# Pairing the products of a seven-product query projection in PSUM banks, and dealing its matmuls out among those of P.V

## The chip, the core and the metric

The kernel runs on one core of a Trainium2 chip. The metric is the device time of one execution in microseconds (us). Before the change it is 1138.15 us, the median of five runs (1136.66 to 1140.64).

## The reference

The input x is 1024 rows of 512 features, all in float32. First comes causal attention with 32 query heads that share 8 key/value heads (groups) of width 128, then a small feed-forward part with routed low-rank experts, each behind a layer norm and added to its input:

```python
q = (hidden_states @ w_q).reshape(B, S, Hkv, g, D)      # 1024 x 512 by 512 x 4096
k = (hidden_states @ w_k).reshape(B, S, Hkv, D)
v = (hidden_states @ w_v).reshape(B, S, Hkv, D)
scores = jnp.einsum('bqhgd,bkhd->bhgqk', q, k) * scale
...
probs = jax.nn.softmax(scores.astype(jnp.float32), axis=-1).astype(q.dtype)
attn = jnp.einsum('bhgqk,bkhd->bqhgd', probs, v)
return attn.reshape(B, S, Hq * D) @ w_o
```

The change concerns the first line, and the order in which its matmuls stand beside those of the last einsum, "P.V".

## The kernel before

**Blocks.** The work is cut into 64 blocks (g, t): group g of 8, and t of 8 tiles of 128 query rows. Groups 0 to 5 run through t = 0 to 7 one after the other (blocks 0 to 47); groups 6 and 7 follow in another order. Block i makes four quarters of scores, j = 0 to 3 (`scores`, L452): a quarter is 32 query rows for each of the group's four heads, 128 rows in all, against the 128t + 32(j+1) keys that the causal mask leaves. TensorE writes a quarter to a tile `s` of two PSUM banks (two such tiles). VectorE adds the mask to the last 32 columns (L472) and takes the negated maximum (L474), ScalarE takes the exponential and its sum (L479), GpSimd the reciprocal (L481). The quarter before is then finished (`finish_scores`): ScalarE multiplies by the reciprocal (L487) and VectorE transposes in 32 x 32 squares into a tile T (L490). After the fourth quarter 16 transfers on SP's queue bring T into a tile K, keys on the partitions (`to_keys`, L500). T and K have one buffer each for even and for odd t.

**P.V** of block i-2 runs in block i (`weighted_values`, L510): t+1 matmuls of 512 columns into one bank `po`, of which there is one. All of them read all parts of K. ScalarE copies the result to attnT (L516).

**The query projection.** A pair is two neighbouring blocks (t even, t odd) of a group, 256 query rows. The odd block i projects the queries of the next pair, m = i // 2 + 1. For m = 2 to 24 (23 pairs, `QW`; blocks 3, 5, ... 47) this is `project_q_halves`, L379: the product of a 2 x 2 block matrix of weights with a 2 x 2 block matrix of x in seven products in place of eight. Product number i multiplies a weight combination `weights["sq", 0][i]` (a11, a12, s4, a22, s1, s2, a21) with a combination of x `weights["tx"][i]` (b11, b21, b22, t4, t1, t2, t3). The sums s1, s2, s4 are made by GpSimd once a group (`combine_q`), t1 to t4 once a pair (`combine_x`, the tile `tx`). A product is four pieces: two halves c of 128 output rows by two steps k of 128 features, each a matmul of 128 columns. It fills half a PSUM bank. Banks come from a pool `pm` of three, which all projections share.

The order is written out by hand: `order` gives for each step n the product, the bank b = 0 to 3 and the half x of it. `merge(n)` is called when step n is complete: at n = 0 ScalarE copies product 0 to both halves of the first half tile of qT (L398); at n = 2 VectorE adds bank 1 (two products, L400); at n = 3 to 6 it adds products by halves (L402, L404, L405, L407, L409). Bank 0 is thus read at n = 0 with one product in it and gets its second at n = 3; bank 2 is read at n = 4 and gets its second product at n = 5.

**Order on TensorE.** For each block the main loop (L810) collects lists of pieces, each with its columns: `q` (the query projection), `other` (key and value projections), `pv`, and in even blocks `o_pair` (the output projection). `weave` deals two lists out by columns. `then` is q in front and the rest behind, and it is run in four shares by columns, one after each quarter of scores. In an odd block of groups 0 to 5, `o`, `o_pair`, `begins` and `ends` are empty, so `rest` is `other` (four value pieces of 256 columns in groups 2 and 4 and in t = 5 and 7 of group 0, nothing in the odd groups) and then `pv` (8, 2, 4 or 6 pieces for t = 1, 3, 5, 7). `combine_o` prepares weights on GpSimd (four subtractions) at the end of block t = 2 of each group from group 1 on; the weights of the next group's queries are loaded at t = 6, those of its output projection at t = 5, on ScalarE's queue. The framework adds the waits; TensorE's order is kept as written (`keep`), that of the other engines is set when the kernel is built.

Of the kernel before, what the change touches and what calls it, by code (L numbers as in the profile page):

```python
# [9 lines left out]
F32 = mybir.dt.float32  # L10
I32 = mybir.dt.int32
AF = mybir.ActivationFunctionType
ALU = mybir.AluOpType
AX = mybir.AxisListType

P = 128
# [6 lines left out]
def kernel(  # L23
# [32 lines left out]
    nc = tc.nc  # L56
# [3 lines left out]
    R = w_q.shape[1] // D // G  # L60
# [5 lines left out]
    PQ = 2 * P  # L66
    SQ = P // R
    NSUB = P // SQ
# [10 lines left out]
    act = ctx.enter_context(tc.tile_pool(name="act", bufs=2))  # L79
# [12 lines left out]
    QW = range(2, N2 // 2 + 1)  # L92
# [4 lines left out]
    def matmul(*args, **kw):  # L97
        keep(nc.tensor.matmul(*args, **kw))  # L98
# [84 lines left out]
    two = (nc.sync, nc.scalar)  # L183
# [77 lines left out]
    def bank(name):  # L261
        return ps_m.tile([P, 512], F32, tag="pm", name=name)
# [38 lines left out]
    vs, kTs, qTs = {}, {}, {}  # L301
# [77 lines left out]
    def project_q_halves(m):  # L379


        g, u = pairs[m]
        hk = KC // 2
        pm = {}

        def half(e, h):

            return both(e)[:, h]

        def both(e):  # L390
            q = qTs[g, u][:, ts(e, NSUB), :, :]
            return q.rearrange("p s (x h) q -> p x s (h q)", x=2)

        def merge(n):
            if n == 0:
                qTs[g, u] = act.tile([P, PQ // SQ, R, SQ], F32, tag="qT", name=f"qT_{g}_{u}")
                one = pm[0][:, 0].unsqueeze(1)
                nc.scalar.copy(both(0), one.to_broadcast([P, 2, NSUB, 2 * SQ]))  # L398
            elif n == 2:
                nc.vector.tensor_tensor(both(0), pm[1], both(0), ALU.add)  # L400
            elif n == 3:
                nc.vector.tensor_tensor(half(1, 0), pm[0][:, 1], half(0, 1), ALU.add)  # L402
            elif n == 4:
                nc.vector.tensor_tensor(half(0, 1), pm[2][:, 0], half(0, 1), ALU.add)  # L404
                nc.vector.tensor_tensor(half(1, 1), pm[0][:, 1], half(0, 1), ALU.add)  # L405
            elif n == 5:
                nc.vector.tensor_tensor(half(1, 0), pm[2][:, 1], half(1, 0), ALU.add)  # L407
            elif n == 6:
                nc.vector.tensor_tensor(half(0, 1), pm[3][:, 0], half(0, 1), ALU.add)  # L409


        order = ((0, 0, 0), (1, 1, 0), (5, 1, 1), (4, 0, 1), (6, 2, 0), (2, 2, 1), (3, 3, 0))

        def piece(n, c, k):
            i, b, x = order[n]
            if c == k == 0:
                if x == 0:
                    whole = bank(f"pq_{g}_{u}_{b}")
                    pm[b] = whole.rearrange("p (x s n) -> p x s n", x=2, s=NSUB)
            assert weights["sq"] == (g,)  # L420
            matmul(
                pm[b][:, x, :, ts(c, SQ)],
                weights["sq", 0][i][:, k, ts(c, D)],
                weights["tx"][i][:, k, :].rearrange("p (s q) -> p s q", q=SQ),
                start=(k == 0),
                stop=(k == hk - 1),
            )
            if c == 1 and k == hk - 1:
                merge(n)

        return [
            (P, lambda n=n, c=c, k=k: piece(n, c, k))
            for n in range(7)
            for c in range(2)
            for k in range(hk)
        ]
# [90 lines left out]
    def project_o(g, t):  # L527


        def finish(pm):  # L530
            nc.vector.tensor_tensor(acc[t], pm, acc[t], ALU.add)
            attnT.pop((g, t))
            ffn_norms(t)

        def term(j):
            return attnT[g, t][:, ts(j, P)], weights["o", g][:, j, :]

        return chained(
            lambda: bank(f"pO_{g}_{t}"), [lambda j=j: term(j) for j in range(R)], finish
        )  # L540
# [68 lines left out]
    def reload_x(t):  # L609
        xt = state["x", t] = ffn.tile([P, H], F32, tag="x", name=f"xr_{t}")  # L610
        load(xt, x[ts(t, P), :])
# [78 lines left out]
    def ffn_store(t):  # L690
        load(out[ts(t, P), :], acc[t])
# [4 lines left out]
    def projections(i):  # L696


        g, t = blocks[i]
        q, other = [], []  # L700
        m = i // 2 + 1
        if i == 0:
            later["q"] = project_q(*pairs[m])
            q = later["q"][: 2 * KC]
        elif i == 1:
            q = later["q"][2 * KC :]
        elif i % 2 and m < len(pairs):
            q = project_q_halves(m) if m in QW else project_q(*pairs[m])
        if i < N2:
            if t == 2:  # L710
                other += project_k(g, 1)
            if t == 6:
                other += project_k(g + 1, 0)
            if g == 0 and t < 2:
                other += [(P * KC, lambda n=TPB + 2 + t: input_turn(n))]
                other += project_v(0, 2 + t)
            elif g % GV == 0 and (g or t >= TPB):
                other += project_v(g // GV, t)
        else:
            n = i - N2  # L720
            for k, what in ((0, (G - 1, 0)), (2, (G - 2, 1)), (3, (G - 1, 1))):
                if n == k:
                    other += project_k(*what)
            for t in {0: (0,), 1: (1,), 2: (2, 3), 3: (4, 5), 4: (6, 7)}.get(n, ()):
                other += project_v(g // GV, t)
        return q, other

    def loads(i):

        g, t = blocks[i]  # L730
        m = (i + 1) // 2 + 1
        if i % 2 == 0 and m < len(pairs):
            for j in range(2):
                load_q(pairs[m][0], j)
        if i < N2:
            if t == 3:
                load_k(g + 1)
            if t == 5 and g + 1 == G - 2:
                load_k(G - 1)
            if t == 6 and (g + 1) % GV == 0:  # L740
                for j in range(2):
                    load_v((g + 1) // GV, j)
            if t == 5:
                load_o(g + 1)
        elif i == N2 + 3:
            load_o(G - 1)
        elif i == N2 + 4:
            load_base("wk", (0, 1))
        elif i == N2 + 5:
            load_base("wv", (2, 3))  # L750
# [15 lines left out]
    def weave(a, b):  # L766

        na, nb = sum(c for c, _ in a), sum(c for c, _ in b)
        merged, at, bt, b = [], 0, 0, list(b)
        for c, f in a:  # L770
            merged.append((c, f))
            at += c
            while b and (bt + b[0][0] / 2) * na <= at * nb:
                bt += b[0][0]
                merged.append(b.pop(0))
        return merged + b
# [21 lines left out]
    def complete(i, *behind):  # L798


        for e in range(2):
            k = i - behind[e % len(behind)]
            if 0 <= k < N and k % 2 == e and blocks[k][0] == G - 1:
                return [blocks[k][1]]
        return []

    def attend(i):
        return weighted_values(*blocks[i])

    for i in range(N):  # L810
        loads(i)
        for t in complete(i, 2):
            reload_x(t)
        for t in complete(i, 7, 8):
            ffn_store(t)
        q, other = projections(i)
        pv = attend(i - 2) if i >= 2 else []
        o, o_pair, ends, begins = [], [], [], []
        for t in complete(i, 3):
            o = project_o(*blocks[i - 3])  # L820
        if i % 2 == 0 and i >= 4 and blocks[i - 4][0] < G - 1:
            o_pair = project_o_pair(*pairs[i // 2 - 2])
        for t in complete(i, 6, 7):
            ends = sum(ffn_out(t), [])
        for t in complete(i, 5):
            begins = ffn_router(t)

        rest = o + weave(o_pair, begins[1:] + other + pv)
        then = begins[:1] + q + ends[:-1] + rest[:4] + ends[-1:] + rest[4:]
        for n in range(NSUB):  # L830
            scores(*blocks[i], n)
            run_share(then, n, NSUB)
            if i % 2 == 0 and n < 2 and i // 2 + 1 in QW:
                (combine_x, combine_q)[n](i // 2 + 1)
        if i == NT:
            prepare_ffn()

        if i >= NT and blocks[i - 2][1] == 0 and blocks[i - 2][0] < G - 1:
            combine_o(blocks[i - 2][0])


    c, d, e, f = (blocks[k][1] for k in (N - 6, N - 5, N - 2, N - 1))
# [60 lines left out]
```

## Time and profile before

| | |
|---|---|
| runs, median (lowest to highest) | 1138.15 us (1136.66 to 1140.64) |
| profiled execution | 1136.66 us, span 1134.9 us |
| mean granted TensorE clock | 0.990 |
| score matmuls (768 records) | 276.3 us |
| P.V matmuls (576 records) | 277.9 us |
| query matmuls of 128 columns (1288 records) | 173.3 us |
| VectorE adds of the 23 projections, L400 to L409 | 15.6 us at 679 ns, the other five groups 9.5 to 9.8 us each at 415 to 424 ns |
| ScalarE copies, L398 | 13.3 us at 579 ns |
| transfers of K, 16 a block | 0.59 us apart on SP's queue, landing 1.7 to 2.5 us after their issue as a rule |

The times of one profiled execution are used for durations; its own time stands in the table beside its span, which runs from its first to its last instruction. A matmul in float32 shows as two records. The end of a matmul is modelled in the records, so their starts say more than their durations; times "at" some number are us from the start of the span.

### The profile page before, as it was taken

Reading aid. Unit: us, or ns where it says so; the run is one execution under the profiler, and the core shown is the slowest. Engines: PE = TensorE matmul, PEld = TensorE weight load, DVE = VectorE, ACT = ScalarE, POOL = GpSimd, SP = SyncE. Lnnn points to the kernel's source line nnn. Section 1 sums busy time; section 2 is a strip of 40 time slices with the busy share of each in tenths; the row PEclk is TensorE's granted clock in tenths of the full one; section 3 lists DMA queues with packets and bytes.
Section 4 is the critical chain, followed back from the end, with each engine's and each line's share of the span. In section 5 each row is a group of like instructions: output and inputs, shape, how many; then the busy total and the mean of one; then the engine's idle time right before and its main releaser. Section 6 shows DMA issues by size and latency. Waiting matters only on the chain.

```text
span 1134.9 us, 14168 instructions
## 1 busy us (share of the span) xinstructions
PE 1073.6 (95%) x4388; PEld 716.6 (63%) x4388; DVE 696.7 (61%) x1423; ACT 449.7 (40%) x962; POOL 331.3 (29%) x649
## 2 busy tenths in 40 slices
PE   8899999999999999999999999899999899999896
PEld 7666666666676666666776666656677456466453
DVE  4476656766566566666566655766336756666755
ACT  2544434444344433444344433444234353343400
POOL 5523334232242424232242424331131111112210
PEclk9999999999999999999999999999999999999998
DMA  6035432446125431455225351464334644453220
GB/s 206 22 93 134 96 84 55 117 122 135 29 68 139 106 87 48 111 132 113 47 60 145 88 111 41 112 152 115 87 96 123 156 111 105 122 129 81 68 71 28
DMA packets 79307, 111.91 MB, mean 99 GB/s; under 512 B 18176, under 2 KB 50960, under 8 KB 79232
## 3 DMA queue, kind: packets, MB, share of 16 engines
q1 hardware_dynamic: 53696, 82.58, 31.5%
q10 hardware_dynamic: 25040, 27.27, 7.7%
q0 software_dynamic: 496, 1.16, 0.3%
q8 instruction: 36, 0.59, 0.2%
q14 instruction: 39, 0.32, 0.1%
HBM read 33.34 MB, written 2.10 MB: 31 GB/s over the span
## 4 chain that ended last, share of the span: by engine, by line
PE 73%; DVE 10%; ACT 4%; SPq 4%; DMA 4%; POOL 2%; issue 2%; ACTq 0%; DVEq 0%; POOLq 0%
PE po L98 18%; PE s L98 16%; PE pq L98 13%; PE pv L98 4%; PE pk L98 4%; SPq L104 4%; PE pa L98 4%; PE pe L98 3%; DVE T L490 3%; ACT p L479 2%; DMA K<-T 2%; PE pb L98 2%; DVE nmax L474 2%; PE pc L98 2%; PE pd L98 2%
## 5 line engine op out<-in xcount | busy, mean ns | idle before, releaser
L479 ACT ACTIVATE p<-s,nmax 128x32 f32<-128x32 f32 (+31 forms) x256 | 179.6, 702 | 487.2 <-DVE nmax L474 452.8
L490 DVE STREAM_TRANSPOSE T<-p 128x128 f32<-128x128 f32 (+7 forms) x256 | 198.7, 776 | 168.0 <-ACT p L487 155.4
L481 POOL TENSOR_TENSOR rec<-total,neg_one 128x1 f32<-128x1 f32 x256 | 143.4, 560 | 494.8 <-ACT p L479 494.5
L98 PE MATMUL s<-kT,qT 128*128 128x512 f32 (+15 forms) x768 | 276.3, 469 | 10.1 <-ACT p L479 10.1
L98 PE MATMUL po<-K,v 128*128 128x512 f32 x576 | 277.9, 596 | 3.8 <-DMA K<-T 3.8
L98 PEld LDWEIGHTS s<-kT,qT 128*128 128x128 f32 x768 | 142.5, 191 | 136.4 <-issue 109.5
L487 ACT ACTIVATE p<-p,rec 128x32 f32<-128x32 f32 (+31 forms) x256 | 185.4, 724 | 3.7 <-POOL rec L481 3.7
L474 DVE TENSOR_REDUCE nmax<-s 128x1 f32<-128x32 f32 (+31 forms) x256 | 180.6, 705 | 7.0
L98 PEld LDWEIGHTS po<-K,v 128*128 128x128 f32 x576 | 107.5, 191 | 77.0 <-issue 67.2
L472 DVE TENSOR_TENSOR s<-s,smask 128x32 f32<-128x32 f32 x256 | 49.3, 193 | 124.6 <-PE s L98 124.1
L98 PE MATMUL pq<-xnT,wq 128*128 128x128 f32 (+1 forms) x656 | 111.0, 321 | 0.0
L98 PEld LDWEIGHTS pq<-xnT,wq 128*128 128x128 f32 x656 | 98.0, 191 | 12.7 <-issue 5.4
L477 POOL MEMSET p<- 128x96 f32 (+2 forms) x192 | 29.1, 152 | 147.3 <-DVE T L490 143.6
L98 PE MATMUL pv<-wv,xnT 128*128 128x256 f32 x256 | 70.3, 389 | 0.8 <-ACT xnT L272 0.8
L98 PE MATMUL pa<-wo,attnT 128*128 128x256 f32 x224 | 62.3, 387 | 2.9 <-ACT hT L272 2.8
L98 PE MATMUL pk<-xnT,wk 128*128 128x512 f32 x128 | 64.5, 593 | 0.0
L516 ACT COPY attnT<-po 128x512 f32<-128x512 f32 x64 | 37.1, 580 | 55.3 <-PE po L98 54.8
L98 PEld LDWEIGHTS pv<-wv,xnT 128*128 128x128 f32 x256 | 48.3, 195 | 10.9 <-issue 2.7
L98 PEld LDWEIGHTS pa<-wo,attnT 128*128 128x128 f32 x224 | 41.0, 190 | 21.5 <-issue 13.4
L98 PE MATMUL pq<-tx,sq 128*128 128x128 f32 x368 | 49.5, 276 | 3.4 <-ACT qT L398 3.4
L158 POOL TENSOR_TENSOR tx<-xnT 128x256 f32<-128x256 f32 x46 | 33.6, 731 | 64.8 <-PE pq L98 64.8
L98 PEld LDWEIGHTS pq<-tx,sq 128*128 128x128 f32 x368 | 46.4, 192 | 8.7 <-issue 4.5
(123 smaller groups left out, 1135.1 us busy)
## 6 DMA issues: line engine op xcount, KB each, us to landing
K<-T SPq DMA_DIRECT2D x128, 128.0 KB, 2.4
K<-T SPq DMA_DIRECT2D x128, 112.0 KB, 2.3
wq<-in_w_q_dram ACTq DMA_DIRECT2D x27, 512.0 KB, 4.8
K<-T SPq DMA_DIRECT2D x128, 96.0 KB, 2.2
K<-T SPq DMA_DIRECT2D x128, 80.0 KB, 2.1
K<-T SPq DMA_DIRECT2D x123, 64.0 KB, 2.0
wo<-in_w_o_dram ACTq DMA_DIRECT2D x28, 256.0 KB, 4.1
K<-T SPq DMA_DIRECT2D x128, 48.0 KB, 1.9
```

The costliest lines, as they stand in the source:

```text
L98: keep(nc.tensor.matmul(*args, **kw))
L104: keep(by.dma_start(dst, src))
L158: nc.gpsimd.tensor_tensor(dst, p, q, ALU.subtract)
L472: nc.vector.tensor_tensor(s[:, n - SQ : n], s[:, n - SQ : n], smask, ALU.add)
L474: nc.vector.tensor_reduce(nmax, s[:, :n], AX.X, ALU.max, negate=True)
L477: nc.gpsimd.memset(p[:, n:full], 0.0)
L479: nc.scalar.activation(p[:, :n], s[:, :n], AF.Exp, bias=nmax, accum_out=total)
L481: pool = nc.gpsimd.tensor_tensor(rec, total, neg_one, ALU.pow)
L487: keep(nc.scalar.mul(p[:, :n], p[:, :n], rec))
L490: nc.vector.transpose(turned[g, t][:, :, j, :, :].rearrange("p b k q -> p k b q"), p[:, :full].rearrange("p (k b q) -> p k b q", b=R, q=SQ),)
L516: nc.scalar.copy(o, po)
```

## The change

Three things change.

1. The products go to the banks two by two, in the order 0, 1 | 5, 6 | 4, 2 | 3. `merge` is called with the bank, when both of its products are complete (bank 3 holds one). No bank is written after it has been read.
2. The merges follow: after bank 0 ScalarE's copy of its first product and one add of its second; after bank 1 two adds, after bank 2 three, after bank 3 one. That is seven adds of 256 columns in place of one of 512 and five of 256.
3. In odd blocks that hold such a projection, the 28 pieces of `q` no longer stand in front of `rest`: they are dealt out by columns among the first three fifths of the pieces of `rest` (`cut`), and the last two fifths follow.

```diff
-        def merge(n):
-            if n == 0:
+        def add(dst, src, to):
+            nc.vector.tensor_tensor(dst, src, to, ALU.add)
+
+        def merge(b):
+
+            one, two = pm[b][:, 0], pm[b][:, 1]
+            if b == 0:
+                nc.scalar.copy(both(0), one.unsqueeze(1).to_broadcast([P, 2, NSUB, 2 * SQ]))
+                add(half(0, 0), two, half(0, 0))
+            elif b == 1:
+                add(half(1, 0), one, half(0, 1))
+                add(half(0, 1), two, half(1, 0))
+            elif b == 2:
+                add(half(1, 1), one, half(0, 1))
+                add(half(1, 0), one, half(1, 0))
+                add(half(1, 0), two, half(1, 0))
+            else:
+                add(half(0, 1), one, half(0, 1))
+
+
+        order = (0, 1, 5, 6, 4, 2, 3)
+
+        def piece(n, c, k):
+            i, b, x = order[n], n // 2, n % 2
+            if n == c == k == 0:
                 qTs[g, u] = act.tile([P, PQ // SQ, R, SQ], F32, tag="qT", name=f"qT_{g}_{u}")
-                one = pm[0][:, 0].unsqueeze(1)
-                nc.scalar.copy(both(0), one.to_broadcast([P, 2, NSUB, 2 * SQ]))
-            elif n == 2:
-                nc.vector.tensor_tensor(both(0), pm[1], both(0), ALU.add)
-            elif n == 3:
-                nc.vector.tensor_tensor(half(1, 0), pm[0][:, 1], half(0, 1), ALU.add)
-            elif n == 4:
-                nc.vector.tensor_tensor(half(0, 1), pm[2][:, 0], half(0, 1), ALU.add)
-                nc.vector.tensor_tensor(half(1, 1), pm[0][:, 1], half(0, 1), ALU.add)
-            elif n == 5:
-                nc.vector.tensor_tensor(half(1, 0), pm[2][:, 1], half(1, 0), ALU.add)
-            elif n == 6:
-                nc.vector.tensor_tensor(half(0, 1), pm[3][:, 0], half(0, 1), ALU.add)
-
-
-        order = ((0, 0, 0), (1, 1, 0), (5, 1, 1), (4, 0, 1), (6, 2, 0), (2, 2, 1), (3, 3, 0))
-
-        def piece(n, c, k):
-            i, b, x = order[n]
-            if c == k == 0:
-                if x == 0:
-                    whole = bank(f"pq_{g}_{u}_{b}")
-                    pm[b] = whole.rearrange("p (x s n) -> p x s n", x=2, s=NSUB)
+            if x == c == k == 0:
+                whole = bank(f"pq_{g}_{u}_{b}")
+                pm[b] = whole.rearrange("p (x s n) -> p x s n", x=2, s=NSUB)
...
-            if c == 1 and k == hk - 1:
-                merge(n)
+            if c == 1 and k == hk - 1 and (x == 1 or n == 6):
+                merge(b)
...
         rest = o + weave(o_pair, begins[1:] + other + pv)
+        if i % 2 and i // 2 + 1 in QW:
+            cut = len(rest) * 3 // 5
+            q, rest = weave(q, rest[:cut]), rest[cut:]
         then = begins[:1] + q + ends[:-1] + rest[:4] + ends[-1:] + rest[4:]
```

## The prediction

> **What bounds the kernel now.** I read the page from the top: busy time by engine, then the chain that ended last, then the list of waits, then single blocks in the timeline.
>
> ```profile
> PE 1073.6 (95%) x4388; PEld 716.6 (63%) x4388; DVE 696.7 (61%) x1423; ACT 449.7 (40%) x962; POOL 331.3 (29%) x649
> PE 73%; DVE 10%; ACT 4%; SPq 4%; DMA 4%; POOL 2%; issue 2%; ACTq 0%; DVEq 0%; POOLq 0%
> ```
>
> TensorE bounds it: it is busy for 95% of the span and holds 73% of the chain. So only the time in which TensorE stands still can be won. The list of waits says how much of that lies at the query products (columns: total us, times, longest):
>
> ```profile
> PE pq L98 <- DVE qT L404: 25.2, 23, 2.3
> PE s L98 <- ACT p L479: 10.1, 12, 2.8
> PE po L98 <- DMA K<-T: 3.8, 1, 3.8
> PE pq L98 <- ACT qT L398: 3.4, 4, 1.2
> ```
>
> 23 waits, one for each projection in seven products: the sixth product goes into the second half of bank 2 and waits until VectorE has read the first half (L404). One of them in the timeline, block g=1, t=3:
>
> ```profile
> 190.78 0.61 PE L98 MATMUL pq<-tx,wq 128*128 128x128 f32 x4
> 193.00 1.16 PE L98 MATMUL pq<-xnT,sq 128*128 128x128 f32 x8 [1.61 <-DVE qT L404]
> ```
>
> In the timeline a float32 matmul is two records, and undisturbed records of 128 columns start 0.107 us apart (16 of pq in 1.79 us, 156.31 to 158.10), of 512 columns 0.429. So the work of a block can be counted from its columns: one 128-column piece 0.215 us, one 512-column piece of P.V 0.86. The length of a block (from its first score matmul to the next block's) less this work is what it loses. The 23 blocks with seven products lose 46.2 us together. That, not 25.2, is the stock: it holds the ends of the matmuls before each wait, the waits on L398, and one clock drop (below).
>
> **The change, part by part.** (1) *The reads of half-filled banks go.* Banks 0, 1 and 2 are read only when both products are in, so the waits on L404 and L398 have nothing left to wait for. (2) *Merges.* One 512-wide add (0.68 us) becomes two of 256 (0.42 each): +0.16 us a projection, 3.7 us of VectorE in all, inside its 39% idle time except in block kind C. ScalarE's copy (0.58) stands two places later in its queue, behind one exponential and one multiply, which come earlier for it. (3) *Order.* The 28 pieces are dealt out over 60% of the other pieces. P.V of block i-2, which began behind all 28 (6.0 us of matmuls), begins in the odd groups after 4 (t=1), 14 (t=3), 7 (t=5) or 5 (t=7) of them. TensorE works its queue in order: if P.V's input is late, the rest of the products and the next quarter's score matmuls wait behind it, and for those VectorE's mask and maximum and ScalarE's exponential. That input, K, is written by 16 transfers of block i-2 on SP's queue. P.V's last piece still ends the block, so the copy of its result and the reuse of K's buffer stay where they were. The last product moves from the middle of the block to some 2 us before its end; the wq loads that wait for it (ScalarE's queue, t=6, issued at 227.8 with the block's start at 227.6) still come after it. In the built kernel SP's order is the same, GpSimd's tx subtractions stand one reciprocal later, and the matmuls are the same.
>
> When does K land? In the block g=1, t=1 (starts at 156.04) it is K of t=7; in g=1, t=5 (starts at 210.41) it is K of t=3. Transfers in these two stretches:
>
> ```profile
> L104 SPq DMA_DIRECT2D K<-T x18: 508/590/596, 147.5 to 159.5; - x18
> ...
> DMA to landing us min/median/max: 1.7/2.4/2.5
> ```
>
> ```profile
> L104 SPq DMA_DIRECT2D K<-T x18: 507/588/592, 203.6 to 217.9; - x18
> ...
> DMA to landing us min/median/max: 1.9/2.0/5.1
> ```
>
> Sixteen issues of 0.59 from 147.5 end at 156.9, landing 159.5. From 203.6 they end at 213.9, and the last lands 3.5 later, at 217.4, because 1 MB of wo moves then. Before, P.V began at 164.2 and 222.8, so nobody waited.
>
> Now the blocks by kind (us, all blocks of the kind; "lost before" from the trace, "lost after" my estimate):
>
> A. 13 blocks: all of the even groups except g=0, t=3, where value projections or more products stand ahead of P.V, and t=7 of the odd groups. First P.V comes 2.6 to 11 us into the block, K has landed, and 3 to 5 pieces (2.1 to 4.3 us) between the last product and the next scores cover the last merge (0.42). Lost before 20.4 (1.6 and 1.4 a block at t=7, 2.4 at t=5, 1.0 at t=1 and t=3), after 2.6 (0.2 each): **-17.8**.
>
> B. t=1 of groups 1, 3, 5. P.V stands after one score matmul (0.27) and 4 pieces (0.86): 156.04+1.13 = 157.2 against 159.5, a wait of 2.3; 2.2 in the other two groups (414.4 and 417.7; 674.4 and 677.7), and I add 0.2 each for merges that come late ahead of the transposes. Lost before 3.3, after 7.3: **+4.0**.
>
> C. t=3 of groups 1, 3, 5. Here VectorE is late by itself: GpSimd prepares wot for 5 us (184.6 to 189.9) ahead of the first reciprocal, so the first transpose is at 191.12. By its order in the built kernel VectorE then does mask, maximum, two adds, transpose (to 194.7), mask, add, maximum, two adds: the query is ready at about 196.9. TensorE, without its stall, would have been through at 194.9 (184.1 + 10.85 of work) and waits 2.0 there for qT; before, the next block began at 197.5. Lost before 7.6, after 6.5: **-1.1**. What L404 cost is late at the end instead.
>
> D. t=5 of groups 1, 3, 5. First P.V after 1.13 + 7 pieces (1.50): 210.4+2.63 = 213.0 against 217.4, a wait of 4.4; 4.5 and 5.4 in groups 3 and 5. K's chain gains some 0.9 and TensorE 0.4 in C, so 0.5 less each. Lost before 10.6, after 12.8: **+2.2**.
>
> Block g=0, t=3 changes one wait for another (4.2 to 4.0); t=0 of odd groups may lose 0.3 each on ScalarE's copy of the previous P.V: **+0.7** together.
>
> E. *The clock.* A gap in TensorE can cost more than its length:
>
> ```profile
> core 0: us, PE busy (x) PEld busy (x) DVE busy (x) ACT busy (x) POOL busy (x), PEclk, DMA share, GB/s
> ...
> 474.40:477.80 3.40, 1.30 (x12) 1.11 (x10) 3.29 (x6) 1.68 (x3) 1.83 (x4) 1.00 0.26 57
> 477.90:481.30 3.40, 3.28 (x8) 2.21 (x9) 0.49 (x2) 0.00 (x0) 0.16 (x1) 0.50 0.56 127
> ```
>
> After an idle stretch of 2.5 us, block g=3, t=5 ran 3.4 us at a granted clock of 0.50 and lost 1.6 us more than its twin in group 1, whose gap was as long (217.2 to 219.7) and whose clock stayed at 1.00. All such stretches in the trace begin a multiple of 3.41 us apart, so what seems to count is how much idle time falls into one such slot: 2.3 did it, 1.95 (at 905) did not. D's gaps of 4 to 5 us put at least 2 us into one slot; part of the slow stretch may fall into the gap itself: 1.2 each (bounds 0 and 1.6). B: 0.6 each, C: 0.45 each, by the share of positions. **+6.8** (bounds 0 and 9 x 1.6 = 14.4).
>
> The Trainium skill ("TensorE: Matmul & The Clock Gate", section "Part 1: The HAM clock gate (the "warmup" mystery)") speaks against P.V's waits: about 3.4 us windows that run freely, half rate after an idle window. By its words only a wholly idle window counts, which a 4.5 us gap holds in about a third of positions; an estimate by that page would charge 1.5 in place of 6.8. The trace differs: 2.5 us sufficed once.
>
> Sum: -17.8 +4.0 -1.1 +2.2 +0.7 +6.8 = **-5.2 us**. The profiled execution took 1136.66 us (span 1134.9), so 1131.5 for such a one; the median of the runs is 1138.15, 1.5 above it, and from that I forecast **1133**.
>
> Unknown sizes: K's landings in B and D could be 1 us off either way (6 us); C could lose nothing (-6.5) or half more (+3); A's remainder is between 0 and the 0.8 a block of an undisturbed handover (g=2, t=3: L404 from 318.26 to 318.69, the next product at 318.74, 0.8 later than its turn), -2.6 to +7.8, and I take 0.2 because those adds have several us; the clock is -6.8 to +7.6. All ends together: 1111 to 1157.
>
> **Rivals.** *R1, the gain comes through*: K lands earlier because VectorE and ScalarE are freed sooner, gaps stay under 2.3 us, no clock drop. For: ScalarE's exponential and multiply stand ahead of its copy now. Against: SP needs 9.5 us for 16 issues whatever the others do. -5.2 -6.8 -6 = -18: **1120** (1111 to 1126). *R2, slower*: P.V waits for K in B and D, with the clock drop behind each gap. Without B, D and the clock the change wins 18.2; these three cost 13.0 in my sum. It decides once they pass 18.2: with a half-clock stretch behind each of nine gaps (14.4) they are 20.6. If K is also 1 us later in those six blocks, 26.6, so +8: **1146** (up to 1157). For: 4.4 us of lateness at 213.0 is read straight from the trace. *R3, it doesn't do what it says in time*: TensorE no longer waits inside a bank but for the same late adds at a bank's reuse (three buffers for four banks and a value bank) or at the next scores, as in C, but in all kinds; then 0.8 a block stays in A (10.4), which gives -10.0 in place of -17.8: +2.6 with E as charged, -0.8 with half of it: **1139**. Against: in A VectorE keeps up, L404 runs at once when its product ends.
>
> **How the numbers follow.** Forecast (1126 to 1135.8) 0.40, R1 0.22, R3 0.15, R2 0.23. 0.2% (2.3 us), about what can be told from no change, puts the bounds at 1135.9 and 1140.4. Faster 0.62, within 0.14, slower 0.24 (a little of R3 is slower). The range leaves out about 0.1 at each end: 1117 to 1147.
>
> **What would show it.** Right: no wait of pq on qT adds; po on DMA K<-T about six times, 2 us at t=1 and 4 us at t=5 of groups 1, 3, 5; s on a qT add three times, some 2 us; PEclk under 1 right behind the long ones; t=7 blocks 1.2 shorter. Wrong: po waits in other blocks, or waits of pq on its bank's adds.

## The result, and the profile after

The changed kernel takes 1140.63 us (median of 32 runs, 1136.91 to 1144.83) against 1138.98 (55 runs, 1135.56 to 1142.27) for the kernel before: a ratio of 1.0014, 95% interval 1.0006 to 1.0021. It is 0.14% slower, less than the 0.2% that the prediction set as its bound for "no change". The forecast was 0.5% faster. The profiled execution took 1142.27 us (span 1140.2, mean granted clock 0.977 after 0.990), 5.6 above that of before; the two stand at different places among their runs (1.6 above its median here, 2.3 below before), so the sums below are held against 5.6 and not against 1.65. The runs of the changed kernel go with the granted clock: the six at 0.982 or 0.983 took 1136.9 to 1139.2, the four at 0.972 or 0.975 took 1141.3 to 1144.5.

Busy time and the chain of waits of the changed kernel:

```profile
PE 1078.6 (95%) x4388; PEld 721.4 (63%) x4388; DVE 692.9 (61%) x1446; ACT 450.8 (40%) x962; POOL 330.5 (29%) x649
...
PE 76%; DVE 6%; SPq 5%; DMA 5%; ACT 3%; POOL 3%; issue 1%; ACTq 0%; POOLq 0%; DVEq 0%
```

VectorE has gone from 10% of the chain to 6%, SP's queue and the DMAs together from 8% to 10%. The same matmuls show 5 us more of busy time. TensorE's list of waits (line 98 is its matmul; the lines behind the diff have moved down by 3):

```profile
PE po L98 <- DMA K<-T: 29.7, 8, 5.5
PE s L98 <- ACT p L482: 13.0, 12, 2.8
```

The 23 waits of pq on L404 and the four on L398 are all gone, and P.V (po) waits for K 29.7 us in place of 3.8: six times in t=1 and t=5 of groups 1, 3 and 5, once in g=0, t=3, and once at the very end. The block g=1, t=5 in the timeline:

```profile
212.12 1.73 PE L98 MATMUL pq<-xnT,wq 128*128 128x128 f32 x14
217.93 2.05 PE L98 MATMUL po<-K,v 128*128 128x512 f32 x2 [4.09 <-DMA K<-T]
219.77 2.55 PE L98 MATMUL s<-kT,qT 128*128 128x512 f32 x4
222.12 0.64 PE L98 MATMUL pq<-xnT,wq 128*128 128x128 f32 x2
```

After seven pieces P.V's first one waits 4.09 us; 21 query pieces that need no K stand behind it. Then the four score records (two of 512 columns and two of 192, for 704 keys; the line names the first one's shape), which take 1.18 undisturbed (2 x 0.429 + 2 x 0.163), need 2.35 until the next matmul starts. The windows say why (the granted clock is the third number from the end of a line):

```profile
core 0: us, PE busy (x) PEld busy (x) DVE busy (x) ACT busy (x) POOL busy (x), PEclk, DMA share, GB/s
153.10:158.90 5.80, 2.75 (x17) 2.06 (x16) 1.60 (x13) 1.36 (x4) 0.67 (x2) 1.00 0.58 129
158.91:162.32 3.41, 3.41 (x15) 3.10 (x14) 0.80 (x3) 0.59 (x1) 0.00 (x0) 0.50 0.13 27
213.52:216.93 3.41, 0.32 (x3) 0.13 (x2) 0.97 (x2) 1.63 (x3) 0.58 (x2) 1.00 0.90 255
216.93:220.34 3.41, 2.41 (x3) 1.18 (x4) 0.00 (x0) 0.00 (x0) 0.10 (x1) 0.50 0.42 95
220.34:223.75 3.41, 3.41 (x12) 2.61 (x11) 1.35 (x3) 0.75 (x2) 0.00 (x0) 0.50 0.54 121
```

In t=1 (153.10 on) one stretch of half clock follows the wait for K, in t=5 two follow each other. All six blocks show this.

Lost time by the kinds of the prediction (length of a block less its matmul work, all blocks of a kind, us). A wait just before the first scores of a block is counted here to that block, not to the one before it as in the prediction; in the kernel before the change the two ways agree.

| | before | forecast | after | pairing alone (e1) | dealing alone (e2) |
|---|---|---|---|---|---|
| A (13 blocks) | 20.4 | 2.6 | 3.6 | 3.4 | 20.8 |
| B (t=1 of g 1, 3, 5) | 3.3 | 7.3 + 1.8 clock | 15.0 | 0.8 | 15.9 |
| C (t=3 of g 1, 3, 5) | 7.6 | 6.5 + 1.4 clock | 4.7 | 4.5 | 6.5 |
| D (t=5 of g 1, 3, 5) | 10.6 | 12.8 + 3.6 clock | 22.2 | 0.8 | 25.2 |
| g=0, t=3 | 4.2 | 4.0 | 4.5 | 3.2 | 5.4 |

The 24 even blocks and g=0, t=1 together lost 11.2 before and 12.8 after, the blocks of the last two groups 23.5 and 23.8. The changes of all rows add up to +5.7, the profiled difference of 5.6.

One part of the table is no loss at all. The prediction counts 0.107 us for a record of 128 columns, but its own row (16 records in 1.79 us) gives 0.112, and that is what undisturbed ones take in all these traces. So a piece is 0.224 us and not 0.215, and each of the 23 blocks shows some 0.25 us as lost that is plain work, in every measured column.

### The profile page after: what moved, and what is told of

It reads as the page before. It is cut to its first block, busy times and chain, and to the rows that moved or that the text cites. A ratio compares the mean times of both kernels' runs of the same rounds, so it can differ in the third digit from the quotient of the medians.

```text
span 1140.2 us, 14125 instructions
## 1 busy us (share of the span) xinstructions
PE 1078.6 (95%) x4388; PEld 721.4 (63%) x4388; DVE 692.9 (61%) x1446; ACT 450.8 (40%) x962; POOL 330.5 (29%) x649
## 4 chain that ended last, share of the span: by engine, by line
PE 76%; DVE 6%; SPq 5%; DMA 5%; ACT 3%; POOL 3%; issue 1%; ACTq 0%; POOLq 0%; DVEq 0%
PE po L98 18%; PE s L98 18%; PE pq L98 15%; SPq L104 5%; PE pv L98 5%; PE pk L98 4%; PE pa L98 4%; PE pe L98 3%; DMA K<-T 3%; PE pO L98 2%; PE pb L98 2%; PE pc L98 2%; PE pd L98 2%; ACT p L482 2%; DVE T L493 2%; PE pf L98 2%
## 5 line engine op out<-in xcount | busy, mean ns | idle before, releaser
L98 PE MATMUL po<-K,v 128*128 128x512 f32 x576 | 287.1, 603 | 29.8 <-DMA K<-T 29.7
L98 PE MATMUL s<-kT,qT 128*128 128x512 f32 (+15 forms) x768 | 279.7, 474 | 13.1 <-ACT p L482 13.0
L98 PEld LDWEIGHTS po<-K,v 128*128 128x128 f32 x576 | 104.8, 193 | 87.0 <-issue 75.8
L98 PE MATMUL pq<-xnT,wq 128*128 128x128 f32 (+1 forms) x656 | 117.9, 326 | 0.0
L98 PEld LDWEIGHTS pq<-xnT,wq 128*128 128x128 f32 x656 | 104.6, 196 | 16.5 <-issue 8.3
L395 DVE TENSOR_TENSOR qT<-pq,qT 128x256 f32<-128x256 f32 x161 | 64.4, 415 | 39.4 <-ACT qT L401 19.3
L98 PE MATMUL pv<-wv,xnT 128*128 128x256 f32 x256 | 73.9, 389 | 0.9 <-ACT xnT L272 0.9
L98 PEld LDWEIGHTS pq<-tx,sq 128*128 128x128 f32 x368 | 53.7, 203 | 9.9 <-issue 9.5
L98 PEld LDWEIGHTS pq<-tx,wq 128*128 128x128 f32 x368 | 50.4, 192 | 12.4 <-issue 11.7
L98 PE MATMUL pq<-tx,sq 128*128 128x128 f32 x368 | 57.7, 286 | 0.0
L98 PEld LDWEIGHTS pa<-wo,attnT 128*128 128x128 f32 x224 | 41.2, 192 | 21.2 <-issue 13.9
```

The source lines that it names most:

```text
L395: nc.vector.tensor_tensor(dst, src, to, ALU.add)
```

## The experiments

Theory T: pairing removes the waits inside banks and wins what the 23 blocks lost; the early place of P.V gives it back, through waits for K in six blocks and the half clock behind each. Rivals: U, that pairing only puts the waits off, to the later merges; V, that the slow stretches are not the idle time's doing. Each kernel was timed beside the kernel before on the same chip.

**e1_pairs_only.** The changed kernel without its third part:

```diff
-        if i % 2 and i // 2 + 1 in QW:
-            cut = len(rest) * 3 // 5
-            q, rest = weave(q, rest[:cut]), rest[cut:]
```

> Products in pairs, merges as in the changed kernel, but the 28 pieces stand in front again and P.V behind them (the three lines of the dealing are taken out). Theory T (the pairing wins what it should, and P.V's early place loses it again to waits for K and to the clock): all 23 blocks lose their waits inside banks; of the 46.2 us some 10 to 13 stay (t=3 of groups 1, 3, 5, where GpSimd and VectorE are late; small rests), so 33 to 36 us less than before, a ratio near 0.970 (1103 to 1108 us); no wait of po on DMA K<-T in blocks 0 to 47, no half clock there. Rival U (the later, more numerous merges are what eats the gain, the dealing is neutral): within 0.3% of the changed kernel, ratio 1.000 to 1.004, with waits of scores or products on the qT adds.

Measured: 1105.18 us, ratio 0.9708 (0.9693 to 0.9724). TensorE's waits of this kernel:

```profile
PE s L98 <- ACT p L482: 13.8, 13, 2.8
PE po L98 <- DMA K<-T: 4.5, 2, 4.0
```

No wait of pq is left and none of P.V in the six blocks. The 23 blocks lose 12.7 us in place of 46.1. U falls: 19 of the 23 blocks show 0.26 us each, which is the miscounted work and no wait; in none of these does a matmul start more than 0.01 us late. What is left is in C and in g=0, t=3. Pairing alone wins 2.9%.

**e2_turns_only.** The reverse: the kernel before, with the three lines above added.

> The dealing alone on the kernel before: old order of products, old merges. T: the K waits and half-clock stretches of the changed kernel's six blocks come in full (37 us lost there against 14 before) on top of the waits on L404 in the 13 other blocks (20 us), which only a P.V piece that happens to stand between two products shortens: 15 to 25 us slower than before, ratio 1.013 to 1.022. U: the dealing is neutral or hides the bank waits behind P.V pieces: ratio 0.985 to 1.000.

Measured: 1165.75 us, ratio 1.0247 (1.0217 to 1.0277), a little more than expected.

```profile
PE po L98 <- DMA K<-T: 28.3, 8, 5.2
PE pq L98 <- DVE qT L404: 21.4, 18, 1.8
```

Both kinds of waits stand side by side; B and D lose 41.1 us in place of 13.9. The dealing alone costs 27.7 us in the 23 blocks, but 37.3 on top of the pairing (12.7 to 50.0): where P.V waits for K, the time that pairing won in the same block is only a longer wait.

**e3_turns_where_k_is_in.** The changed kernel, dealing left out in t=1 and t=5 of groups 1, 3 and 5 alone:

```diff
-        if i % 2 and i // 2 + 1 in QW:
+        late = blocks[i][0] % 2 and blocks[i][1] in (1, 5)
+        if i % 2 and i // 2 + 1 in QW and not late:
```

> The changed kernel, but in t=1 and t=5 of groups 1, 3, 5 the products stand in front of P.V as before the change. T: these six blocks lose about 1 us each in place of the 37 us together, so 33 to 36 us less than the changed kernel, ratio to the kernel before 0.969 to 0.974, about as the pairs alone: where K is in, the dealing gains and loses next to nothing. U: unchanged against the changed kernel, 1.000 to 1.004.

Measured: 1107.35 us, ratio 0.9733 (0.9712 to 0.9753). B and D lose 0.26 a block. In the other 17 blocks the dealing wins nothing and costs next to nothing, but for g=0, t=3, where P.V waits for K as well (4.5 against 3.2 without dealing). So all but about 2 us of the loss comes from six blocks.

**e4_filled_gaps.** The changed kernel with spare matmuls in front of the six waits: 12 and 18 more pieces, which compute product 0's first half again, at t=1 and t=5 of groups 1, 3 and 5.

```diff
+    FILL = {(1, 1): (2, 6), (1, 5): (6, 9)}
...
+        place, times = FILL.get((blocks[2 * m - 1][0] % 2, blocks[2 * m - 1][1]), (0, 0))
+        more = [(0, lambda k=k: again(k)) for _ in range(times) for k in range(hk)]
+        return work[:place] + more + work[place:]
```

> The changed kernel, and in t=1 and t=5 of groups 1, 3, 5 the first four or so pieces are followed by repeats of product 0's first half (the same values into the same place of the bank): 12 extra pieces (2.6 us) at t=1, 18 (3.9 us) at t=5, which fit into the gap that ended at 157.5 and 217.9 in the changed kernel. Extra work of 19 us that should cost nothing but keep the clock up. T: the waits for K shrink to under 1.5 us each, K's landing and so the restart of TensorE stay where they are, and the half-clock stretches of these six blocks go: 12 to 15 us less than the changed kernel, ratio to the kernel before 0.988 to 0.991. Rival V (the slow stretch behind the wait isn't the clock but late engines, or the clock goes down for another reason): same as the changed kernel, or up to 19 us slower.

Measured: 1131.51 us, ratio 0.9935 (0.9914 to 0.9955). The kernel does some 20 us more matmuls (90 pieces of 0.224) and takes some 9 us less than the changed one. The windows over the two blocks of group 1:

```profile
core 0: us, PE busy (x) PEld busy (x) DVE busy (x) ACT busy (x) POOL busy (x), PEclk, DMA share, GB/s
153.00:160.00 7.00, 6.73 (x47) 5.58 (x46) 2.21 (x13) 1.36 (x4) 0.83 (x3) 1.00 0.64 139
212.00:222.00 10.00, 9.73 (x75) 8.62 (x74) 3.66 (x7) 2.80 (x6) 0.82 (x3) 1.00 0.69 182
```

The clock stays at 1.00 where it fell to 0.50. V falls: the same transfers are under way and only the idle time is gone. The gain was expected at 12 to 15; in the profiled execution it is 13.3, though that one also has a half-clock stretch in g=0, t=3, and its six blocks are 12.7 us shorter in spite of the added work. By the medians it is 9, and the ratio lies above the expected 0.988 to 0.991: the profiled execution had a mean clock of 0.994, the other three 0.987 to 0.989. Where those three were slowed was not recorded.

**e5_two_queues.** The changed kernel with K earlier in the six blocks:

```diff
+                soon = g < 6 and t in (3, 7) and (g + (t == 7)) % 2
-                to_keys(g, t, by=three if (g, t) == blocks[-1] else three[:1])
+                to_keys(g, t, by=three if (g, t) == blocks[-1] else (nc.sync, nc.gpsimd) if soon else three[:1])
```

> The changed kernel, pairing and dealing as they are; only the 16 transfers of K that the six late blocks wait for (the K of t=7 ahead of groups 1, 3, 5 and of t=3 in them) are issued by SP's and GpSimd's queues in turn, 8 each, in place of 16 on SP's. Theory T (what is lost is lost to K's landing, and to the half clock behind the gap that the wait leaves): 8 issues of 0.59 us take 4.7 us less than 16, so K lands some 4.7 us earlier, 152.7 in place of 157.4 in the first block, where its turn is at 154.4, and about 212.8 to 214.4 in the second, where its turn is at 213.6. The waits go, and with them the slow stretches: the six blocks lose 37.2 us in the changed kernel and would lose 2 to 6, so the ratio to the kernel before is 0.972 to 0.976. Rival W (it is the dealing in these blocks itself, P.V between products whose merges are late, and K only happens to be named): the waits move to the merges, ratio 0.99 to 1.001. A cost that could blur it: GpSimd's reciprocals stand behind its eight issues.

Measured: 1119.65 us, ratio 0.9827 (0.9810 to 0.9844): between the two theories' ranges, because the six blocks part. K of t=3, the transfers that D waits for:

```profile
L104 SPq DMA_DIRECT2D K<-T x8: 508/590/602, 201.2 to 205.5; - x8
L104 POOL DMA_DIRECT2D K<-T x8: 498/498/540, 201.6 to 205.2; - x8
```

It has landed at 208.3, 7.1 us after its first issue, in place of 13.8 (203.7 to 217.5) on one queue, where the last transfers met the loads of the output weights; the three blocks D lose 0.8 in all and not 22.2, as T says. K of t=7 is twice as large (16 transfers of 128 KB): its first landing comes at 147.6 and the last at 156.6, 9.1 us for 2 MB, against 9.9 on one queue. My expectation counted issues alone, and here halving them on each queue brought little. So 2.2 us of waiting stay in each B, and these make a comparison that was not planned. The slots of 3.41 us around the wait in g=1, t=1 and in g=3, t=1:

```profile
core 0: us, PE busy (x) PEld busy (x) DVE busy (x) ACT busy (x) POOL busy (x), PEclk, DMA share, GB/s
155.10:158.51 3.41, 1.76 (x10) 1.31 (x11) 0.31 (x1) 0.77 (x3) 0.68 (x2) 1.00 0.30 66
158.51:161.92 3.41, 3.41 (x27) 2.93 (x26) 1.54 (x5) 1.41 (x4) 0.55 (x1) 1.00 0.12 26
404.27:407.68 3.41, 1.14 (x9) 0.92 (x8) 0.79 (x4) 1.05 (x4) 0.68 (x2) 1.00 0.62 142
407.69:411.10 3.41, 3.41 (x13) 2.57 (x12) 0.00 (x0) 0.29 (x1) 0.00 (x0) 0.50 0.13 27
```

The waits are as long (2.22 and 2.27). The first lies across two slots and costs nothing more; the second has 1.14 us of busy time in its slot, and in the next one TensorE gets through 13 records in place of 27. The blocks lose 2.7 and 4.4: the half clock alone costs 1.7, half of a slot.

**e6_wot_by_quarters.** What e1 still loses is 1.5 us in each block C, where the fourth quarter's scores wait for ScalarE's exponential. Here GpSimd's four subtractions for wot are issued one by one behind the quarters of t=3 (core of the edit, on e1):

```diff
+            if steps:
+                steps.pop(0)()
...
-            combine_o(blocks[i - 2][0])
+            steps = combine_o(blocks[i - 2][0])
```

> The pairing alone (no dealing), and GpSimd's four subtractions for the output weights (1.27 us each) no longer together at the end of t=2 but one behind each quarter of scores of t=3, in groups 1 to 5. Theory T (the 1.5 us still lost in each t=3 of groups 1, 3, 5 are the fourth quarter's scores waiting for a score tile, whose exponential is late because the reciprocals stand behind 5 us of subtractions): these three blocks lose 0.3, 3.6 us less in all than with the pairing alone, ratio to the kernel before 0.967 to 0.969. Rival X (the tile is late for another reason, VectorE's five adds among the masks): nothing changes, ratio 0.970 to 0.972.

Measured: 1104.80 us, ratio 0.9700 (0.9684 to 0.9716). C loses 4.5 as before. The edit did not do what it says: in the profile the four subtractions still stand together, 178.78 to 184.1 in g=1, t=3, since the order of that engine is set when the kernel is built. So it doesn't tell the two theories apart. But it showed the place of the wait, in TensorE's timeline and then ScalarE's:

```profile
187.71 1.13 PE L98 MATMUL s<-kT,qT 128*128 128x512 f32 x2 [0.98 <-ACT p L482]
```

```profile
186.90 0.66 ACT L482 ACTIVATE p<-s,nmax 128x480 f32<-128x480 f32 x1 [1.62 <-DVE nmax L477]
```

The scores start right behind the exponential of the *third* quarter (480 columns), which reads the other half of the same tile.

**e7_own_score_tile.** e1, and in t=3 each quarter takes a tile of its own:

```diff
-        if t < TPB and j % 2:
+        if t < TPB - 1 and j % 2:
```

> The pairing alone (no dealing), and in the blocks t=3 each quarter of scores takes a tile of its own, where for t under 4 the second and the fourth quarter go into the other half of the tile that the quarter before them took. In the run with the subtractions by quarters the fourth quarter's scores of g=1, t=3 began at 187.71, right behind the third quarter's exponential (186.90 to 187.56), which reads the other half of the same tile. Theory Y (the 1.25 us wait in each t=3 of groups 1, 3, 5 is this: a matmul waits for the reader of the other half of its tile, as the query products did inside a bank): with a tile of its own the fourth quarter follows the second's exponential, which ended at 183.7, and the wait goes: 3.6 us less than with the pairing alone, ratio to the kernel before 0.967 to 0.969. Rival Z (the tiles are also short by count, two for four quarters): the wait moves to the next block's first scores or to the third quarter, ratio 0.970 to 0.974.

Measured: 1105.33 us, ratio 0.9695 (0.9681 to 0.9710): the same as e1 within the intervals. The mechanism holds and the gain doesn't: the wait goes from every block C (0.75 in all, from 4.5) and from g=0, t=3 (0.25 from 3.2), and in the next block this stands:

```profile
188.56 1.24 PE L98 MATMUL s<-kT,qT 128*128 128x512 f32 x4
189.63 1.54 PE L98 MATMUL pa<-wo,attnT 128*128 128x256 f32 x6
192.46 1.10 PE L98 MATMUL po<-K,v 128*128 128x512 f32 x2 [1.29 <-DMA K<-T]
```

K of t=2, issued from 181.0 to 190.5, lands at 192.4. The even blocks lose 18.5 in place of 13.1. The edit also changes t=3 of the last two groups: P.V of the very last block waits 8.9 us for K in place of 4.0, and the blocks of these groups and what follows lose 2.5 more.

**e8_own_tile_two_queues.** e7, and K of t=2 in groups 1, 3 and 5 from two queues:

```diff
+                soon = g in (1, 3, 5) and t == 2
-                to_keys(g, t, by=three if (g, t) == blocks[-1] else three[:1])
+                to_keys(g, t, by=three if (g, t) == blocks[-1] else (nc.sync, nc.gpsimd) if soon else three[:1])
```

> The kernel before this one (pairing alone, own score tiles at t=3), and the 16 transfers of K of t=2 in groups 1, 3, 5, for which P.V in t=4 now waits 1.5 us (K lands at 192.4, its turn is at 190.9), from SP's and GpSimd's queues in turn. Theory (the wait that went from t=3 came back at t=4 because K's 16 issues, 181.0 to 190.5, set the pace): K lands 2 to 4 us earlier, the waits go, 1.3 us in each of three groups: 4 us less, ratio 0.965 to 0.967. Rival (GpSimd's 4 us of issues stand ahead of reciprocals and of its subtractions for tx, so that scores or products wait instead): 0.969 to 0.974.

Measured: 1105.36 us, ratio 0.9691 (0.9677 to 0.9704). K lands at 188.7, 3.7 us earlier, and its wait in t=4 is gone. Now the first scores of that block wait:

```profile
189.78 1.24 PE L98 MATMUL s<-kT,qT 128*128 128x512 f32 x4 [1.58 <-DVE qT L395]
190.85 1.54 PE L98 MATMUL pa<-wo,attnT 128*128 128x256 f32 x6
192.23 1.11 PE L98 MATMUL po<-K,v 128*128 128x512 f32 x2
```

This is the wait that the prediction foresaw for C: VectorE's merges are late. The rival named the price beforehand; whether GpSimd's four us of issues made the merges late or they would have been late anyway was not told apart. Three waits lie one behind the other there, and each edit shows the next. No version in this study is faster than the pairing alone, e1, by more than the intervals.

## Why the prediction was wrong, point by point

- **Removal of the waits in banks (1).** Right: none is left, and e1 shows what it is worth by itself, 33.4 us in the 23 blocks.
- **Merges (2).** Right: seven adds of 415 ns on average, hidden; e1 refutes a cost of them.
- **A.** Right: -16.8 for -17.8. Of the 3.6 us that are left, some 3.3 are the miscounted work (0.25 a block), so next to nothing is lost.
- **C.** The sum was right in sign and too small, -3.0 for -1.1 with no clock loss where 1.4 was charged, but by another mechanism: in the changed kernel the 1.05-us wait of this block is not one for qT; the fourth quarter waits for the exponential of the third in the other half of its tile. In e7 the wait for K comes behind it, and in e8 the foreseen one for qT, though GpSimd's issues may have had a part in that.
- **B and D, the waits for K.** The mechanism is right, at the places named, and the sizes were short: without the slow stretches the six blocks lose 9.9 (B) and 14.4 (D), of which 9.1 and 13.6 are the waits, forecast 7.3 and 12.8. In B K landed 17.4 us after the block before began, not 16.7 as in the trace of before, which the forecast had taken over.
- **E, the clock. This is the step that failed most.** 13.0 us for 6.8. The slot rule of the prediction was right; how it was priced was not. B was charged 0.6 a block "by the share of positions": in all three, the slot held 2.1 to 2.7 us of idle time and the half clock came each time (5.1 for 1.8). D was charged 1.2, with part of the slow stretch falling into the gap; it does fall there in part, but then a second one follows (7.9 for 3.6). The price of a stretch held: 1.7 us each in B, where it was busy throughout, and 2.2 to 2.9 for each pair in D. All nine come near the upper bound that the prediction gave (14.4), although it thought of C for three of the nine. There is chance in it: the 2.1 us of g=1, t=1 lie where other slots went either way (last section).
- **The rest.** g=0, t=3, the even blocks and the last groups changed by +2.2, where +0.7 was charged; why the even blocks lose 1.6 more was not looked into.

With these, -5.2 becomes: +6.2 (E), +4.1 (B, D), +1.0 (A), -1.9 (C), +1.5 (the rest) = +5.7, against 5.6 in the profiled execution. That is one execution of each kernel, and the pair overstates the clock: its granted clocks are 0.990 and 0.977, while the medians of the runs with a clock on record are 0.987 (34 runs of the kernel before) and 0.979 (33 of the changed one). Between the medians of the times the forecast missed by 6.9 and not by 10.8; how the smaller miss divides among the terms no trace shows.

The rival that decided is R2: its three costs, 13.0 in the forecast's sum, measured 23.4 (6.6 in B, 3.8 in D, 13.0 for the clock), above its turning point of 18.2. It named the mechanism and the point; its time of 1146 assumed K a microsecond later still. The forecast did not take apart the two halves of the change: e1 and e2 show -2.9% and +2.5%, so the sum was the small difference of two large terms, and 10 us missed in one of them turned its sign.

The Trainium skill's rule that the prediction weighed ("TensorE: Matmul & The Clock Gate", section "Part 1: The HAM clock gate (the "warmup" mystery)") names an idle window before the half rate. Here it came after slots with 1.14 us of busy time in 3.41, and B's gaps of about 3 us fill no whole slot; the measurement decides, and the estimate by that page (1.5) would have been further off than 6.8.

## What to carry to other kernels

Filling a wait by moving other work ahead is safe only if that work's own inputs have landed: on an engine that works in order, read the landing time of the moved work's last transfer against its new turn, block by block, and leave out the blocks where it is late. Price a TensorE gap by the slot that it falls into, not by its length, and charge the whole stretch at half clock (1.7 us here) for every slot that is mostly idle, and a second one if the wait reaches into the first. When a change has two parts with opposite effects, cost each by itself first: their difference tells little about either.

## What the runs showed of the hardware that was not expected

- **The granted clock goes by slots, with a narrow threshold.** In all ten traces of this study, from 130 to 1080 us, I summed TensorE's idle time in each 3.41-us slot from the matmuls' starts and columns. Every full-speed slot with 2.28 us or more of idle time was followed by one at 0.50; none with 2.06 or less was; between 2.08 and 2.20 six were and four were not. So in these traces the turning point lies near 2.1 us, some six tenths of a slot.
- **A half-clock slot that is itself partly idle is followed by another.** In the three blocks D the slow slot began with 1.1 to 2.6 us of the same wait, and the next slot was at 0.50 too (216.93 to 223.75); in the three blocks B it was all busy and full speed came back after 3.41 us. In the same stretch of all ten traces, every half-clock slot with 0.81 us or more of idle time was followed by another, and none with 0.53 or less.
- **Two queues help small transfers and hardly large ones.** K of 1 MB landed 7.1 us after its first issue, 13.8 on one queue, where its last six transfers met the loads of the output weights; K of t=2 (0.75 MB) took 8.1 in e8 and 11.3 in e7. K of 2 MB gained 0.8 to 0.9 us, and SP's last three issues then came 1.7 to 1.9 us apart in place of 0.6. (On one queue an issue takes 0.59 us, but they start 0.63 apart: the 16 of g=0, t=7 at 145.19 to 154.66.) Whether the queue or the moving of the data holds them back was not tried.
- **Eight transfers issued by GpSimd keep it busy for 4 us** (498 ns each), and a reciprocal stands right behind them: in e5 they take 201.64 to 205.69, and the next reciprocal starts at 205.70.
